# Key products shared between VectorE and GpSimd, initial states written behind the products, five pair buffers for the values, and attention outputs in the banks of the scores

## The chip, the cores and the metric

The kernel runs on one core of one Trainium2 chip. A core has a matrix engine (TensorE, PE in the profile; its weight loads are listed apart as PEld), a vector engine (VectorE, DVE), an activation engine (ScalarE, ACT), a general engine (GpSimd, POOL) and a queue that here issues all transfers (SyncE, SP). They run side by side, each works through its own instructions in order, and they meet through semaphores. SBUF is the on-chip memory of 128 partitions; matmul results land in PSUM, of which the kernel's four pools take 2 + 4 + 1 + 1 banks. The metric is the time of one execution on the device in microseconds (us).

## The reference, cut to what matters

Two layers follow each other on 16 sequences of 112 tokens of width 512.

```
# layer 0: cross-attention, 16 heads of 32, context of 375 rows
a = layer_norm(ctx);  Q, K, V = x @ Wq.T, a @ Wk.T, a @ Wv.T
x = x + tanh(gate) * (softmax(Q @ K.T * scale, masked) @ V) @ Wo.T

# layer 1: recurrence with a 16 x 16 state per head, 32 heads
xk, xw, xv, xr, xg = five token-shift mixes of layer_norm(x)
w = exp(-exp(decay(xw)));  r, k, v, g = projections of xr, xk, xv, xg
for t:  out_t = r_t . (u * k_t v_t^T + s);   s = k_t v_t^T + w_t[:, None] * s
x1 = x + (group_norm(out) * silu(g)) @ Wo.T
out = x1 + sigmoid(mix_r @ Wfr.T) * (relu(mix_k @ Wfk.T)**2 @ Wfv.T)
```

What matters here is the loop over `t`. The state starts from rows of the context (`s0`), each step adds the outer product of keys and values, and the output reads the state with `r`.

## The kernel before, in words

The 16 sequences form four groups (g) of four, 448 columns each. Two Python generators are woven into one program. `attention()` makes the first layer for all groups, and `recurrent(g)` the second for one group. The recurrence yields numbers, and after each the attention is advanced by as much work as `FILL[g]` times that number (1.2, 1.2, 0.9 and 0.0). The last group runs without attention beside it. TensorE's order is this program's order. The other engines' orders are laid down by the framework's planner, which may put an instruction of theirs ahead of another one of the program.

**Attention.** Per sequence b and quarter m of the heads, `scores` (L217) takes four banks of the pool `ps_s`, which has four, and writes four score tiles (L231). VectorE adds the mask and takes the minimum (L241, one instruction per head with its accumulator read), ScalarE does the exponential (L244). One round later `transposed` (L250) turns the weights in three pieces through the same pool (L254, copies L260 and L262), and one round after that `outputs` (L265) multiplies them with the values (L272) and ScalarE copies the result (L276). Units of other work (context transposes, keys, values, query and output projections) are put between. All these, and `outputs` too, take their bank from the pool `ps_mm`, which has two.

**Recurrence.** After layer norm and mixes a group has 16 steps n: four chunks c of 128 features by four pieces e. The decay products of a chunk are put in a PSUM tile (L507). In a step every partition holds one (head, i) pair, and the four rows q of a buffer hold four j. The columns are time, so the recurrence is a scan along the columns:

- `spread(n)` (L516): four transfers (L524) read value rows back from DRAM and broadcast each to 16 partitions, 223.5 KB each. Then ScalarE copies the initial states into the first column of each sequence (L528).
- `scans(n)` (L532): for each pair of rows VectorE multiplies the values with the keys in place (L544), scans each row (L548), and GpSimd multiplies the pair with the receptances (L552).
- `summed(n)` (L556): TensorE sums over i (L562), and every fourth time the result goes on (L568).

The buffers of four rows are two for the values (`kva`, `kvb`) and two for the states (`sta`, `stb`), taken by n % 2. In the loop the order was: the scans of step n, a projection of chunk c + 1, the spread of n + 1, the sums of n - 1, and the group norm pieces `centred`, `scaled`, `gated` of chunk c - 1.

Projections take their weights from a pool of slabs (L101), eight deep, loaded by the same SP queue as the spreads, the context (L91), the mask row (L221) and the value rows' way out to DRAM (L483).

## Time and profile before

| | |
|---|---|
| median of 3 runs | 1715.88 us (1714.5 to 1718.19) |
| the profiled execution's own time | 1713.49 us |
| its span | 1711.6 us |
| TensorE busy | 1417.8 us (83%) |
| VectorE busy | 960.9 us (56%) |
| ScalarE busy | 602.8 us (35%) |
| GpSimd busy | 442.3 us (26%) |
| mean granted TensorE clock | 0.902 |
| key products (L544) | 128 instructions, 94.0 + 99.3 us |
| scans (L548) | 256 instructions, 130.9 + 130.2 us |
| receptance products (L552) | 128 instructions, 144.5 + 141.0 us |
| initial-state copies (L528) | 64 instructions, 7.0 + 6.9 us |

The steps of the four groups lie at about 355 to 550, 750 to 955, 1150 to 1340 and 1490 to 1627 us. Before 355 there is attention alone, then the first layer norm and mixes. Between the others lie the end of one group, the feed-forward part and the start of the next, with attention between. A row of a timeline gives start, duration, engine, line, operation and operands, and in brackets the idle time of the engine before it with what ended it. A row of waits gives the sum, the number of times and the longest.

### The profile page before, as it was taken

The numbers are of one execution on the slowest core, as the hardware profiler recorded it, in microseconds if no ns is written. First come the engines' busy times: TensorE is split into PE (matmuls) and PEld (weight loads), VectorE is DVE, ScalarE is ACT, GpSimd is POOL, SyncE is SP. The second block draws the span as 40 slices with busy tenths as digits, with TensorE's granted clock in tenths as the row PEclk, the third lists the DMA queues.
The fourth block names the chain that finished last, engine by engine and source line by source line (L and its number), as shares of the span: only waits on it lengthen the run. The fifth ranks groups of instructions, "written<-read, shape, count | busy, mean of one in ns | idle before, by whom it ended". The sixth has DMA issues, their size and how long they took to land.

```text
span 1711.6 us, 17731 instructions
## 1 busy us (share of the span) xinstructions
PE 1417.8 (83%) x6272; PEld 701.5 (41%) x6272; DVE 960.9 (56%) x1660; ACT 602.8 (35%) x1324; POOL 442.3 (26%) x290
## 2 busy tenths in 40 slices
PE   6899999887878889897787889988777987967658
PEld 3455554443333454444343445444332543422124
DVE  1244333668766252549777333467877543599932
ACT  2455454423343352433333442342232532112231
POOL 0000001323434111123354110223444120355510
PEclk9899999999988989998998989988798998889689
DMA  7100010043321113014332012104332112144211
GB/s 220 59 20 20 20 48 22 20 126 106 118 95 54 57 49 111 20 32 136 117 117 90 29 55 85 37 18 149 116 106 84 33 50 76 55 161 146 90 37 46
DMA packets 74887, 129.61 MB, mean 76 GB/s; under 512 B 7680, under 2 KB 47616, under 8 KB 74544
## 3 DMA queue, kind: packets, MB, share of 16 engines
q1 hardware_dynamic: 74800, 128.50, 23.7%
q8 instruction: 49, 0.80, 0.2%
q14 instruction: 38, 0.31, 0.1%
HBM read 121.13 MB, written 7.34 MB: 75 GB/s over the span
## 4 chain that ended last, share of the span: by engine, by line
PE 47%; DVE 22%; DMA 17%; ACT 7%; issue 5%; POOL 2%; SPq 1%; DVEq 0%; ACTq 0%; POOLq 0%
PE pv L180 8%; DMA ctx<-in_ctx 6%; PE pk L170 5%; DMA kvb<-vd 5%; DVE stb L548 5%; DVE sta L548 5%; DMA kva<-vd 4%; PE pfk L122 3%; PE pfv L122 3%; PE pfr L122 3%; PE po L122 3%; ACT pr L244 3%; PE pt L254 3%; PE pq L122 3%; PE pp L122 2%
## 5 line engine op out<-in xcount | busy, mean ns | idle before, releaser
L170 PE MATMUL pk<-aT,wk 128*128 128x375 f32 x512 | 204.3, 549 | 29.5 <-DVE qT L297 11.2
L552 POOL TENSOR_TENSOR sta<-sta,r 128x896 f32<-128x896 f32 x64 | 144.5, 2271 | 250.0 <-DVE sta L548 245.9
L180 PE MATMUL pv<-wv,aT 128*125 128x512 f32 x384 | 190.3, 644 | 22.1 <-DVE o L573 6.2
L552 POOL TENSOR_TENSOR stb<-stb,r 128x896 f32<-128x896 f32 x64 | 141.0, 2220 | 156.6 <-DVE stb L548 156.6
L244 ACT ACTIVATE pr<-pr,mn 112x375 f32<-112x375 f32 x256 | 152.3, 596 | 71.9 <-DVE mn L241 71.4
L241 DVE CUSTOM_DVE_ANT_0 pr<-ps,mb 112x375 f32<-112x375 f32 x256 | 126.4, 542 | 76.8 <-PE ps L231 76.5
L170 PEld LDWEIGHTS pk<-aT,wk 128*128 128x128 f32 x512 | 107.7, 220 | 103.2 <-issue 27.0
L254 PEld LDWEIGHTS pt<-ident,pr 112*125 112x125 f32 x768 | 110.2, 206 | 64.3 <-issue 34.8
L548 DVE TENSOR_TENSOR_SCAN stb<-wp,kvb 128x448 f32<-128x448 f32 x128 | 130.2, 1068 | 9.3 <-PE acc L562 9.3
L548 DVE TENSOR_TENSOR_SCAN sta<-wp,kva 128x448 f32<-128x448 f32 x128 | 130.9, 1070 | 5.3 <-ACT kva L528 5.3
L254 PE MATMUL pt<-ident,pr 112*125 112x112 f32 x768 | 119.0, 294 | 15.7 <-DVE xm L441 15.7
L544 DVE TENSOR_TENSOR kva<-kva,k 128x888 f32<-128x888 f32 x64 | 94.0, 1475 | 45.7 <-DMA kva<-vd 45.1
L180 PEld LDWEIGHTS pv<-wv,aT 128*125 128x125 f32 x384 | 74.7, 204 | 108.9 <-issue 83.3
L544 DVE TENSOR_TENSOR kvb<-kvb,k 128x888 f32<-128x888 f32 x64 | 99.3, 1561 | 23.8 <-DMA kvb<-vd 23.7
L445 POOL TENSOR_TENSOR xm<-xm,xa 128x448 f32<-128x448 f32 x48 | 56.3, 1194 | 179.2 <-DVE xm L441 175.2
L262 DVE COPY prT<-pt 125x448 f32<-125x448 f32 x80 | 49.4, 617 | 86.6 <-PE pt L254 86.4
L231 PE MATMUL ps<-kT,qT 32*112 32x375 f32 x512 | 79.9, 552 | 16.5 <-ACT prT L260 11.1
L260 ACT COPY prT<-pt 125x448 f32<-125x448 f32 x112 | 59.3, 530 | 87.8 <-PE pt L254 87.8
L156 PE MATMUL pa<-ident,ctx 125*128 125x125 f32 x192 | 39.4, 323 | 54.9 <-DVE ctx L141 16.9
L135 DVE BATCH_NORM_STATS2 st<-ctx 125x6 f32<-125x512 f32 x48 | 31.2, 677 | 92.1 <-DMA ctx<-in_ctx 92.1
L175 ACT COPY kT<-pk 128x375 f32<-128x375 f32 x64 | 30.0, 469 | 127.4 <-PE pk L170 127.4
L223 POOL TENSOR_SCALAR mb<-mrow 112x375 f32<-112x375 uint8 x16 | 10.7, 671 | 246.5 <-DVE mn L241 163.9
(143 smaller groups left out, 2158.2 us busy)
## 6 DMA issues: line engine op xcount, KB each, us to landing
kva<-vd SPq DMA_DIRECT2D x128, 223.5 KB
kvb<-vd SPq DMA_DIRECT2D x128, 223.5 KB
ctx<-in_ctx SPq DMA_DIRECT2D x16, 750.0 KB
wo<-in_wo SPq DMA_DIRECT2D x32, 256.0 KB
wq<-in_wq SPq DMA_DIRECT2D x16, 256.0 KB
wv<-in_wv SPq DMA_DIRECT2D x16, 256.0 KB
wk<-in_wk SPq DMA_DIRECT2D x16, 256.0 KB
wr<-in_wr SPq DMA_DIRECT2D x16, 256.0 KB
```

The costliest lines, as they stand in the source:

```text
L122: nc.tensor.matmul(ps[:, :N], w[:, k, :], rhs[:, k, :], start=(k == 0), stop=(k == NC - 1))
L170: nc.tensor.matmul(pk[:, :S], wk[:, k, m * P : (m + 1) * P], aT[:, k, :], start=(k == 0), stop=(k == NC - 1),)
L180: nc.tensor.matmul(pv[:SC, :], aT[:, k, c * SC : (c + 1) * SC], wv[:, k, :], start=(k == 0), stop=(k == NC - 1),)
L231: nc.tensor.matmul(ps[:T, :S], qT[r : r + HD, m, t0 : t0 + T], kT[r : r + HD, :], start=True, stop=True,)
L241: nc.vector.tensor_tensor_reduce(pr, pss[hh][:T, :S], mb, 1.0, 3.0e38, ALU.add, ALU.min, mn)
L244: nc.scalar.activation(pr, pr, AF.Exp, bias=mn, scale=-1.0, accum_out=dens[b][:, h : h + 1])
L254: nc.tensor.transpose(pt[:SC, hh * T : (hh + 1) * T], prs[hh][:, c * SC : (c + 1) * SC], ident[:T, :T])
L260: nc.scalar.copy(prT, pt[:SC, :N])
L445: engine.tensor_tensor(xm[f][:, c, :], xm[f][:, c, :], xa[:, c, :], ALU.add)
L544: nc.vector.tensor_tensor(pair, pair, k_prev.unsqueeze(1).broadcast_to([P, 2, GB, T - 1]), ALU.mult)
L548: nc.vector.tensor_tensor_scan(st[:, q, :], w_ps[c], kv[:, q, :], 0.0, ALU.mult, ALU.add)
L552: nc.gpsimd.tensor_tensor(pair, pair, rs[c].unsqueeze(1).broadcast_to([P, 2, N]), ALU.mult)
```

## The change

- The slabs are six deep instead of eight.
- `outputs` takes its bank from `ps_s` instead of `ps_mm`.
- The value buffers are cut to pairs: two from `kva`, two from `kvb`, and a fifth, `kvc`. Step n uses pairs 2n and 2n + 1, modulo five.
- `spread` issues transfers only. The initial states are no longer copied by ScalarE.
- A new `products(n)` multiplies the first pair of a step on VectorE and the second on GpSimd, each followed on the same engine by a copy of its initial states into the first columns.
- `scans(n)` has no products any more.
- In the loop the spread of n + 1 comes before the scans of n, and the products of n + 1 come after the projection, where the spread was.

```diff
-    slabs = pool("slabs", 8)
+    slabs = pool("slabs", 6)
...
-        po = mm_tile(f"po_{b}_{m}")
+        po = ps_s.tile([P, 512], F32, tag="s", name=f"po_{b}_{m}")
...
-        kvs = [wide("xa", f"kva_{g}"), wide("kv", f"kvb_{g}")]
+        kva, kvb = wide("xa", f"kva_{g}"), wide("kv", f"kvb_{g}")
+        kvc = big.tile([P, 2, N], F32, tag="kvc", name=f"kvc_{g}")
+        kvs = [kva[:, 0:2], kva[:, 2:4], kvb[:, 0:2], kvb[:, 2:4], kvc]
...
-            kv = kvs[n % 2]
...
             for q in range(NQ):
+                kv = kvs[(2 * n + q // 2) % len(kvs)]
                 nc.sync.dma_start(
-                    kv[:, q, 1:N],
+                    kv[:, q % 2, 1:N],
...
-            nc.scalar.copy(
-                kv.rearrange("p q (b t) -> p q b t", t=T)[:, :, :, 0], s0[:, c, e : NS : NQ, :]
-            )
+        def products(n):
+            c, e = divmod(n, NQ)
+            k_prev = ks[c].rearrange("p (b t) -> p b t", t=T)[:, :, 0 : T - 1]
+            for p, engine in enumerate((nc.vector, nc.gpsimd)):
+                kv4 = kvs[(2 * n + p) % len(kvs)].rearrange("p q (b t) -> p q b t", t=T)
+                engine.tensor_tensor(
+                    kv4[:, :, :, 1:T], kv4[:, :, :, 1:T],
+                    k_prev.unsqueeze(1).broadcast_to([P, 2, GB, T - 1]), ALU.mult,
+                )
+                engine.tensor_copy(
+                    kv4[:, :, :, 0], s0[:, c, 8 * p + e : 8 * p + e + 5 : NQ, :]
+                )
...
-            for q0 in (0, 2):
-                pair = kv4[:, q0 : q0 + 2]
-                nc.vector.tensor_tensor(
-                    pair, pair, k_prev.unsqueeze(1).broadcast_to([P, 2, GB, T - 1]), ALU.mult
-                )
-                for q in (q0, q0 + 1):
+            for p in range(2):
+                kv = kvs[(2 * n + p) % len(kvs)]
+                for q in range(2):
...
         spread(0)
+        products(0)
         for n in range(NQ * NC):
...
+            if n + 1 < NQ * NC:
+                spread(n + 1)
             scans(n)
...
             if n + 1 < NQ * NC:
-                spread(n + 1)
+                products(n + 1)
```

## The prediction

> **What bounds the kernel now.** I read the page's slices first, then busy time by stage, then waits, then single rows. The slices show TensorE nearly full, with its clock sagging where the scans run.

> ```profile
> PE   6899999887878889897787889988777987967658
> ...
> PEclk9899999999988989998998989988798998889689
> ```

> By stage (columns: stretch, its length, busy time and count of PE, PEld, DVE, ACT, POOL, granted clock, transfers' share, GB/s):

> ```profile
> 60.00:300.00 240.00, 222.53 (x1321) 126.92 (x1322) 95.71 (x285) 118.02 (x291) 13.61 (x21) 0.95 0.09 27
> 355.00:550.00 195.00, 153.89 (x703) 73.16 (x702) 150.47 (x207) 69.53 (x159) 77.43 (x37) 0.88 0.32 106
> 550.00:750.00 200.00, 176.44 (x808) 91.85 (x806) 79.96 (x192) 80.18 (x172) 36.97 (x36) 0.96 0.17 52
> 750.00:955.00 205.00, 166.57 (x759) 80.57 (x759) 151.30 (x215) 71.66 (x165) 78.86 (x38) 0.88 0.32 103
> ...
> 1150.00:1340.00 190.00, 152.81 (x654) 70.95 (x652) 141.28 (x185) 59.38 (x138) 78.72 (x41) 0.87 0.32 104
> 1490.00:1627.00 137.00, 93.92 (x246) 29.78 (x247) 132.24 (x118) 28.87 (x55) 70.59 (x34) 0.81 0.41 134
> ```

> TensorE idles 41, 38 and 37 us in the first three groups' steps (rows 2, 4, 5), 117 us together, at a clock of 0.87 to 0.88. In row 1 it idles 7%. The last group's steps are VectorE's: 132 of 137 us busy, and from 1490.0 to 1626.6 us it makes 16 steps of 8.54 us. So the change is worth what it does to TensorE's waits in three stretches and to VectorE's chain in the fourth. Who is late in the three stretches?

> ```profile
> ACT kva L528 <- DMA kva<-vd: 130.9, 26, 9.4
> ...
> ACT kvb L528 <- DMA kvb<-vd: 113.9, 26, 6.6
> ```

> ScalarE stands 245 us at the head of an initial-state copy, waiting for value rows, with its other work behind. Two ScalarE rows and two TensorE rows of the timeline show what that costs:

> ```profile
> 830.07 0.22 ACT L528 COPY kva<-s 128x16 f32<-128x16 f32 x1 [7.29 <-DMA kva<-vd]
> 830.18 0.53 ACT L481 COPY v<-pv 128x448 f32<-128x448 f32 x1
> ...
> 826.34 0.76 PE L272 MATMUL po<-prT,v 125*32 125x112 f32 x24
> 830.76 4.18 PE L170 MATMUL pk<-aT,wk 128*128 128x375 f32 x8 [3.66 <-ACT v L481]
> ```

> The value eviction L481 sits behind the copy, its bank stays taken, TensorE stops 3.66 us, and its next eight matmuls take 4.18 us where the same row elsewhere takes 2.70.

> **ScalarE's copies go.** 64 copies of 0.22 us free 14 us of an engine with room: nothing by itself. The wait counts. I laid each TensorE stall of the three stretches over ScalarE's waits for value rows: they overlap for 14, 13 and 11 us, 38 together. The rest of the 117 us hangs on exponentials, on VectorE, on context loads. I take three quarters, since another late engine often stands behind the first: -28. From below nothing is gained if ScalarE's next item is late too; from above 38 plus some 10 of backlog worked off after the wait. [...] By the rows, 473 us of busy TensorE times (1 - 0.88/0.90) is 10.5 us for two hundredths of clock. [...]

> **Outputs in the score banks.** Gain: the output copy L276, late behind four exponentials, no longer holds one of two `ps_mm` banks. TensorE waits for it 27 us in the three stretches (6 already in the 38) and 17 us elsewhere. I take -8 and -15. Loss: per round the score pool is now asked for 4 + 1 + 3 banks, with four there, so the outputs want the bank of the round's first scores, and cannot start before VectorE has read it:

> ```profile
> 127.24 0.90 PE L231 MATMUL ps<-kT,qT 32*112 32x375 f32 x8
> 128.06 0.78 PE L272 MATMUL po<-prT,v 125*32 125x112 f32 x24
> ...
> 128.15 0.55 DVE L241 CUSTOM_DVE_ANT_0 pr<-ps,mb 112x375 f32<-112x375 f32 x1 [3.63 <-PE ps L231]
> ```

> Here outputs start at 128.06 and the read ends at 128.70: a new wait of 0.64 us, with an idle VectorE. Going through all 62 outputs so, the read ends later than the start by 61 us in sum: 28 outside the three stretches, 33 inside. Behind the waiting outputs is the whole of TensorE. Outside I count all, +28, as nothing covers it. Inside, about half falls on stalls there already (the 5.2 us at 826.34 meets the 3.66 us above): +14. Bounds: 0 and 33, more if VectorE gets later.

> **Products and states, spread earlier, five pairs.** VectorE loses 64 products and gains 64 copies of 8 elements; GpSimd gains 64 products and 64 copies. The prices:

> ```profile
> L544 DVE TENSOR_TENSOR kva<-kva,k x64: 1048/1084/2996, 360.1 to 1612.9; 128x888 f32<-128x888 f32 x64
> ...
> L552 POOL TENSOR_TENSOR sta<-sta,r x64: 2070/2082/2926, 366.1 to 1618.2; 128x896 f32<-128x896 f32 x64
> ...
> L141 DVE TENSOR_SCALAR ctx<-ctx,mv,rs x48: 533/542/2300, 16.2 to 1148.2; 125x512 f32<-125x512 f32 x48
> ```

> A product is 1.05 us on VectorE when free, and 2.07 on GpSimd by L552, of the same kind and nearly the same size; its broken rows might make it 2.5. Small copies: 0.16 us on VectorE (by L402, 128x4), 0.2 on GpSimd (by L283, 203 ns). The maxima above are 1.8 to 1.9 us over the minima: VectorE has stood behind GpSimd for most of a GpSimd instruction. [...] By the uncontended rows the last group's step on VectorE would be 4.02 (scans) + 1.05 + 0.16 + about 1.2 (others) = 6.4 us, a saving of 16 x 2.1 = 34. [...] I take 8.35: 16 x (8.54 - 8.35) = -3, between -34 and +6. [...]

> In the first three groups a step takes 12 us, so both engines have room. VectorE sheds 25 us of products per group and up to 21 us of waits for rows, since a pair's transfers now wait for scans 1.5 to 2 steps back instead of one, and rows take 3 to 6.5 us to land in the chain's entries. It pays with about 1.5 us per small copy shut out and 1 us per step for GpSimd's product. I call that even: 0, from -20 to +30. GpSimd's product can queue behind the receptance products, the gate product (L593), mask and spread work (L223, L287), and VectorE's third scan waits for it. Behind that scan sits L241, and behind L241 the exponentials and outputs. Behind the first product on VectorE stand the same.

> **Queues.** The four transfers of a spread (3.5 us of SP when issued together) move ahead of a slab load and, once per chunk, of the value rows' way out (L483), which is due four steps later. With six slabs, a load would go out when the sixth projection back has ended; over all 160 projections the nearest still leaves 14.9 us before first use. Such a load moves 256 KB, a spread 894 KB in about 5 us, so it is there in time: 0. POOL's queue issues no transfer.

> **Sum.** -28 - 6 - 8 + 14 - 15 + 28 - 3 = -18, on the profiled 1713.5 us: 1695.5. The median shown is 2.4 us above that execution, so **1698 us**. Its own range, with the halves I took varied, is 1680 to 1712.

> **Rivals.** (a) Outputs wait longer (slower, **1740**). One mechanism: VectorE reaches L241 later, since GpSimd shuts it out more. If all 61 us count and no bank wait is saved, the sum is -28 - 6 + 61 - 3 = +24. It turns slower once the outputs' waits cost 37 us net. For it: 33 us inside the stretches arise with VectorE 77% busy. Against: VectorE's waits for rows, part of that lateness, should go. [...] (c) The stalls fall much further (**1670**), as the coupling of ScalarE, VectorE and TensorE dissolves: 28 us more. For: the stretches between idle 11 to 12%. Against: a third of the stalls has no part in the value rows.

> **Chances.** Forecast 0.42, (a) 0.26, (b) 0.15, (c) 0.17. This kernel's measurement tells about 0.2% (3.4 us) from no change. Faster: 0.36 + 0.01 + 0.03 + 0.17 = 0.57; same: 0.04 + 0.03 + 0.04 = 0.11; slower: 0.02 + 0.22 + 0.08 = 0.32. The range leaves out the ends of (a) and (c): **1655 to 1745**.

> **What would show it.** Right: no ScalarE wait for `kva` or `kvb`; TensorE idle near 28 us per stretch at a clock near 0.90; L272 waiting for L241 some 0.6 us in quiet rounds; GpSimd about 160 us busier. Wrong: L272 waiting over 60 us in all; L548 waiting for GpSimd in most steps; the last group's step far from 8.35 us; a transfer of slabs in TensorE's waits.

## The result: no measurable change

The changed kernel takes 1711.35 us (median of 20 executions, 1697.12 to 1721.35) and the kernel before, beside it, 1712.85 us (1706.84 to 1720.83). The ratio is 0.9986 with a 95% interval of 0.9965 to 1.0007. The prediction had 1698 us and a clear gain as the likeliest case. The profiled execution took 1710.53 us, with a span of 1708.6 us and a mean granted clock of 0.901.

The gain was not absent, it was given back. The same stretches as before, in columns of the same order (stretch, length, busy time and count of PE, PEld, DVE, ACT and POOL, granted clock, share of the transfers, GB/s); the stretches are shifted to the changed kernel's own steps:

```profile
60.00:300.00 240.00, 212.78 (x1241) 121.13 (x1242) 91.22 (x273) 113.78 (x278) 13.26 (x20) 0.95 0.09 26
364.00:559.00 195.00, 160.10 (x720) 76.14 (x720) 136.16 (x208) 70.15 (x147) 112.41 (x70) 0.87 0.33 107
...
754.00:959.00 205.00, 168.83 (x758) 80.98 (x757) 137.70 (x215) 70.41 (x147) 112.33 (x70) 0.86 0.31 103
...
1487.00:1624.00 137.00, 96.25 (x266) 32.84 (x266) 118.41 (x118) 27.47 (x41) 114.17 (x66) 0.85 0.44 141
```

In the quiet stretch TensorE is now idle 27.2 us instead of 17.5. In the steps (second and third row) it is idle 35 and 36 us, with the clock lower than before (0.87 and 0.86 against 0.88), where about 28 us and 0.90 were expected. In the last group VectorE is busy 118 us and GpSimd 114, and the same 137 us hold 20 matmuls more.

The waits of the changed kernel (engine, line and tile, what it waited for: sum, times, longest):

```profile
PE po L272 <- DVE mn L241: 77.1, 38, 7.1
...
POOL kva L538 <- DMA kva<-vd: 72.6, 9, 20.5
...
DVE kva L538 <- DMA kva<-vd: 34.7, 14, 5.0
DVE kvb L538 <- DMA kvb<-vd: 30.6, 9, 5.7
...
DVE kvc L542 <- DMA kvc<-vd: 15.3, 3, 5.4
```

ScalarE's 245 us for value rows are gone, as forecast. But VectorE's waits for rows, which were to fall, rose from 69 us to 105 us (all its lines for `kva`, `kvb` and `kvc` together), and the outputs' new wait for L241 is 77 us, over the 60 that the prediction named as a sign against it. Three rows of the changed kernel's timeline for VectorE and two for TensorE show one place where both occur:

```profile
829.46 2.04 DVE L542 COPY kvb<-s 128x8 f32<-128x8 f32 x1
...
833.93 1.08 DVE L538 TENSOR_TENSOR kvc<-kvc,k 128x888 f32<-128x888 f32 x1 [2.35 <-DMA kvc<-vd]
...
835.00 0.54 DVE L241 CUSTOM_DVE_ANT_0 pr<-ps,mb 112x375 f32<-112x375 f32 x1
...
835.60 1.35 PE L272 MATMUL po<-prT,v 125*32 125x112 f32 x24 [6.85 <-DVE mn L241]
836.88 4.36 PE L170 MATMUL pk<-aT,wk 128*128 128x375 f32 x8
```

VectorE spends 2.04 us on a copy of 8 elements and stands 2.35 us at the head of a product whose rows have not landed. L241 is the next of its instructions that matter to TensorE; it starts at 835.00, and the outputs at 835.60, after 6.85 us without work on TensorE. So the wait for rows is a third of this stall. Whether it is what costs the time, the experiments have to tell.

### The profile page after: what moved, and what is told of

It is laid out like the page before. It is cut to its first block, busy times and chain, and to the rows that moved or that the text cites. A ratio compares the mean times of both kernels' runs of the same rounds, so it can differ in the third digit from the quotient of the medians.

```text
span 1708.6 us, 17672 instructions
## 1 busy us (share of the span) xinstructions
PE 1413.5 (83%) x6272; PEld 697.1 (41%) x6272; DVE 904.6 (53%) x1660; ACT 594.1 (35%) x1260; POOL 584.5 (34%) x418
## 4 chain that ended last, share of the span: by engine, by line
PE 49%; DVE 21%; DMA 18%; ACT 5%; issue 4%; POOL 3%; SPq 1%; DVEq 0%; POOLq 0%; ACTq 0%
DMA ctx<-in_ctx 7%; PE pv L180 7%; PE pk L170 6%; DVE sta L557 5%; DVE stb L557 4%; DMA kvb<-vd 4%; PE pfk L122 3%; PE pfv L122 3%; PE pfr L122 3%; DMA kva<-vd 3%; PE po L122 3%; PE pp L122 3%; PE pq L122 3%; PE pt L254 2%; PE ps L231 2%
## 5 line engine op out<-in xcount | busy, mean ns | idle before, releaser
L170 PE MATMUL pk<-aT,wk 128*128 128x375 f32 x512 | 207.3, 556 | 23.9 <-DVE qT L297 13.5
L180 PE MATMUL pv<-wv,aT 128*125 128x512 f32 x384 | 175.8, 603 | 5.2 <-DVE g L601 4.3
L561 POOL TENSOR_TENSOR stb<-stb,r 128x896 f32<-128x896 f32 x64 | 137.1, 2163 | 75.8 <-DVE stb L557 73.9
L241 DVE CUSTOM_DVE_ANT_0 pr<-ps,mb 112x375 f32<-112x375 f32 x256 | 126.3, 540 | 65.6 <-PE ps L231 65.6
L170 PEld LDWEIGHTS pk<-aT,wk 128*128 128x128 f32 x512 | 108.5, 222 | 100.0 <-issue 29.0
L254 PEld LDWEIGHTS pt<-ident,pr 112*125 112x125 f32 x768 | 106.4, 199 | 66.5 <-issue 36.4
L272 PE MATMUL po<-prT,v 125*32 125x112 f32 x1536 | 58.1, 291 | 77.9 <-DVE mn L241 77.1
L180 PEld LDWEIGHTS pv<-wv,aT 128*125 128x125 f32 x384 | 69.5, 189 | 83.1 <-issue 74.3
L223 POOL TENSOR_SCALAR mb<-mrow 112x375 f32<-112x375 uint8 x16 | 10.0, 628 | 252.8 <-DVE mn L241 165.8
L538 POOL TENSOR_TENSOR kva<-kva,k 128x888 f32<-128x888 f32 x28 | 58.0, 2072 | 99.5 <-DMA kva<-vd 72.6
L272 PEld LDWEIGHTS po<-prT,v 125*32 125x32 f32 x1536 | 40.4, 121 | 122.7 <-DVE mn L241 114.2
L231 PE MATMUL ps<-kT,qT 32*112 32x375 f32 x512 | 80.8, 563 | 9.6 <-DVE prT L262 6.1
L571 PE MATMUL acc<-sta,consts 128*32 128x448 f32 x256 | 46.9, 658 | 32.9 <-POOL sta L561 16.5
L122 PE MATMUL pr<-xm,wr 128*128 128x448 f32 x128 | 63.2, 646 | 6.1 <-DVE o L582 6.1
```

Of the source, the lines that this page charges most:

```text
L122: nc.tensor.matmul(ps[:, :N], w[:, k, :], rhs[:, k, :], start=(k == 0), stop=(k == NC - 1))
L170: nc.tensor.matmul(pk[:, :S], wk[:, k, m * P : (m + 1) * P], aT[:, k, :], start=(k == 0), stop=(k == NC - 1),)
L180: nc.tensor.matmul(pv[:SC, :], aT[:, k, c * SC : (c + 1) * SC], wv[:, k, :], start=(k == 0), stop=(k == NC - 1),)
L231: nc.tensor.matmul(ps[:T, :S], qT[r : r + HD, m, t0 : t0 + T], kT[r : r + HD, :], start=True, stop=True,)
L241: nc.vector.tensor_tensor_reduce(pr, pss[hh][:T, :S], mb, 1.0, 3.0e38, ALU.add, ALU.min, mn)
L254: nc.tensor.transpose(pt[:SC, hh * T : (hh + 1) * T], prs[hh][:, c * SC : (c + 1) * SC], ident[:T, :T])
```

## The experiments

The recorded expectations give theories letters, in the order in which they were formed, and say in words what each holds: first the outputs' new wait, then GpSimd's share and the small copies that it shuts out, last (D) the fifth pair and VectorE's order. "The run with the outputs back" is the first experiment.

To place a difference, each span is cut at TensorE's milestones: a group's steps run from its first value projection of the recurrence to the first matmul of its output projection. The steps of the first three groups are added up; the rest is the span less all four groups' steps. Single profiles differ by some 5 us in a stage, so verdicts go by the ratios. Each ratio is to executions of the kernel before on the same chip, so medians of two rows are not set against each other; a difference of ratios is turned into us with 1713 us.

| kernel | median us | ratio to before, 95% | span | steps of groups 1 to 3 | last group | rest | VectorE's waits for rows |
|---|---|---|---|---|---|---|---|
| before | 1712.85 | 1 | 1711.6 | 658.2 | 156.5 | 897.0 | 69 |
| changed | 1711.35 | 0.9986 [0.9965, 1.0007] | 1708.6 | 644.8 | 147.1 | 916.7 | 105 |
| e1 outputs back | 1686.10 | 0.9849 [0.9808, 0.9890] | 1685.7 | 650.4 | 146.8 | 888.5 | 110 |
| e2 outputs alone | 1722.38 | 1.0052 [1.0032, 1.0073] | 1720.4 | 645.2 | 156.9 | 918.3 | 71 |
| e3 products on VectorE | 1712.28 | 1.0010 [0.9988, 1.0032] | 1705.0 | 631.6 | 160.9 | 912.5 | 43 |
| g1 states behind, alone | 1680.23 | 0.9838 [0.9811, 0.9866] | 1676.4 | 633.8 | 156.9 | 885.7 | 44 |
| f1 four pairs, outputs back | 1664.46 | 0.9737 [0.9701, 0.9773] | 1669.6 | 630.7 | 147.4 | 891.5 | 36 |
| h2 changed, four pairs | 1684.63 | 0.9836 [0.9809, 0.9862] | 1682.1 | 616.3 | 147.9 | 917.9 | 42 |
| f6 order held, one step | 1649.77 | 0.9652 [0.9627, 0.9677] | 1650.7 | 613.4 | 147.2 | 890.1 | 11 |
| f7 order held behind scans | 1670.74 | 0.9775 [0.9750, 0.9801] | 1666.5 | 622.1 | 156.2 | 888.2 | 8 |
| f8 changed, held | 1679.63 | 0.9824 [0.9803, 0.9846] | 1677.7 | 600.8 | 157.8 | 919.1 | 7 |
| f9 four pairs, held | 1676.54 | 0.9776 [0.9750, 0.9803] | 1675.5 | 625.6 | 154.1 | 895.8 | 8 |
| f10 f6 + last copies on ScalarE | 1645.44 | 0.9611 [0.9585, 0.9637] | 1646.3 | 615.1 | 140.3 | 890.9 | 9 |
| f11 f10 + outputs in steps | 1634.65 | 0.9586 [0.9559, 0.9612] | 1628.8 | 597.1 | 140.3 | 891.4 | 7 |

### Outputs back in the shared banks

```diff
-        po = ps_s.tile([P, 512], F32, tag="s", name=f"po_{b}_{m}")
+        po = mm_tile(f"po_{b}_{m}")
```

> The changed kernel with one edit undone: the outputs take their bank from the two-bank pool again. Theory A (the outputs' wait for VectorE ate the gain): the 77 us in which TensorE waits for L241 before the outputs go, some 25 to 35 us of waits for the output copy come back, and the kernel falls to 1665 to 1690 us. Theory B (the wait for the value rows only moved from ScalarE to VectorE and GpSimd, so nothing was won to be eaten): only the quiet rounds gain, 10 to 15 us, 1697 to 1702 us, and TensorE still idles 33 us or more in each of the first three groups' steps.

Ratio 0.9849, against 0.9986 with the outputs in the score banks: this edit alone costs the changed kernel 0.0137 of 1713 us, 23 us. The `po` wait for L241 is gone from its waits, and the rest of the span falls from 916.7 to 888.5 us. Theory A's range holds, but not its place: the steps do not get shorter (644.8 to 650.4 us), and TensorE still idles over 42 us in each, as B has it.

### The outputs' edit alone, on the kernel before

The same line, the other way, in the kernel before.

> The kernel before with one edit: the outputs in the score banks. Theory A: slower by 20 to 45 us, 1733 to 1758 us, with over 60 us of waits of the outputs for L241. Theory B: slower by the quiet rounds' share, about 10 us, 1720 to 1725 us, since inside the steps TensorE was stopped anyway.

Ratio 1.0052, 9 us slower, as theory B had it. The new wait is the same as in the changed kernel, though VectorE makes all products here and GpSimd's share is the old one:

```profile
PE po L272 <- DVE mn L241: 78.8, 38, 7.7
```

So the 77 us of waiting in the changed kernel do not come from GpSimd's products. The stages show where it costs: the rest grows by 21 us, while the steps take 13 us less.

### All products on VectorE

```diff
-            for p, engine in enumerate((nc.vector, nc.gpsimd)):
+            for p, engine in enumerate((nc.vector, nc.vector)):
```

> The changed kernel with both products and both small copies on VectorE. Theory C (GpSimd shutting VectorE out costs as much as VectorE sheds): within 5 us of the changed kernel in the first three groups, the small copies seldom over 0.2 us. Against C: VectorE's extra 25 us of products per group make the first three groups' steps longer, 1720 to 1735 us in all. Either way the last group's steps go from 147 us back to 155 us or more.

Ratio 1.0010: no difference from the changed kernel that these intervals show. Two things cancel. The last group takes 13.8 us more, so GpSimd's half does pay there. The steps of the other groups take 13 us less although VectorE has 48 products more there, and its waits for rows are 43 us instead of 105. That pointed away from shutting out and toward the waits.

### States behind the products, alone

```diff
-            nc.scalar.copy(
-                kv.rearrange("p q (b t) -> p q b t", t=T)[:, :, :, 0], s0[:, c, e : NS : NQ, :]
-            )
...
                     pair, pair, k_prev.unsqueeze(1).broadcast_to([P, 2, GB, T - 1]), ALU.mult
                 )
+                nc.vector.tensor_copy(
+                    kv.rearrange("p q (b t) -> p q b t", t=T)[:, q0 : q0 + 2, :, 0],
+                    s0[:, c, 4 * q0 + e : 4 * q0 + e + 5 : NQ, :],
+                )
```

> The kernel before with one edit: the initial states are copied by VectorE behind each pair's product instead of by ScalarE ahead of it; everything else as before. My prediction's term for ScalarE's wait and the clock was -34 us: 1675 to 1685 us if it is right. Theory B (the wait for rows is VectorE's too, and only moves): 1700 us or more, since VectorE already stands at these rows with its products and TensorE's stalls inside the steps end a little later at the next engine.

Ratio 0.9838, 28 us faster with this one edit. It is the gain that the prediction put first, in its total. In its parts it is not: TensorE's idle time in the steps of groups 1 to 3 falls by 11 us only (127 to 115), its busy time there by 13, and the rest of the span is 11 us shorter, which is not clear of the scatter between profiles. VectorE's waits for rows fall as well, from 69 to 44 us.

### Four pairs instead of five

```diff
-        kvc = big.tile([P, 2, N], F32, tag="kvc", name=f"kvc_{g}")
-        kvs = [kva[:, 0:2], kva[:, 2:4], kvb[:, 0:2], kvb[:, 2:4], kvc]
+        kvs = [kva[:, 0:2], kva[:, 2:4], kvb[:, 0:2], kvb[:, 2:4]]
```

With the outputs back in the shared banks:

> The kernel with the outputs back in their own banks, and four pair buffers instead of five. Theory D (with five pairs the planner puts products and small copies up to two steps ahead of their scans, where VectorE stands for rows not due yet and in front of L241): VectorE's waits for value rows fall well below the 110 us of the five-pair form, and the time falls by 5 to 15 us, to 1671 to 1681 us. Against D: the rows are asked for half a step later and arrive later, VectorE and GpSimd wait more, 1690 to 1700 us.

In the changed kernel itself:

> The changed kernel with four pair buffers instead of five and nothing else. Theory D (the fifth pair lets the planner put products two steps ahead, and VectorE stands there): faster than the changed kernel by what the four pairs gave with the outputs back, 10 to 20 us, 1690 to 1702 us, with VectorE's waits for value rows well under 105 us. Against D (the gain belonged to that other placing): 1705 to 1715 us.

A buffer less is faster in both settings: 0.9737 against 0.9849 (19 us) and 0.9836 against 0.9986 (25 us). TensorE's order of instructions is the same row by row. What moves are the waits; with four pairs GpSimd waits longer for rows and VectorE shorter (first kernel):

```profile
POOL kva L537 <- DMA kva<-vd: 104.8, 22, 26.4
...
DVE kva L537 <- DMA kva<-vd: 20.5, 12, 2.4
DVE kvb L537 <- DMA kvb<-vd: 15.3, 11, 2.6
```

GpSimd's 150 us of waiting cost nothing that is seen; with VectorE's 110 goes the longer time. The order of instructions suggests why. VectorE's products (P), copies of states (C) and scans (S) of steps 0 to 5 in the first group, with the number of L241 rows between (two for each head, with the accumulator read):

```
planner's order, five pairs:  P0 C0 S0 P1 C1 P2 S1 [4] C2 P3 [4] C3 C4 P4 S2 [8] P5 C5 S3 ...
held to one step (f6):        P0 C0 S0 P1 C1 P2 S1 [4] C2 P3 [4] C3 S2 [6] P4 [2] C4 S3 P5 C5 S4 ...
held behind scans (f7):       P0 C0 S0 P1 C1 S1 P2 [6] C2 [2] S2 [6] P3 [2] C3 S3 ...
```

A fifth pair comes free earlier, so the planner puts P4 ahead of S2. Counted in the trace of the changed kernel, by how many scans have started before a product, 32 of VectorE's 48 products in the first three groups stand more than one step ahead of their own scans, and 66 of the 73 us for which these 48 wait lie before those 32. With four pairs none stands so far ahead. This was still a reading; the next three runs change the order and keep the five pairs.

### VectorE's order held

The first lets a product stand at most one step ahead, the second and third put it behind the last scan of the step before. The edges set the order of issue on VectorE only. Five pairs and their transfers stay, the first two with the outputs back. In the trace of the first, against the run with the outputs back, 78 of VectorE's 1660 rows stand elsewhere in the order, 7 of GpSimd's 418, 3 of ScalarE's 1260, one transfer and no matmul. Under the stricter hold more follows: in the third, against the changed kernel, 34 of GpSimd's rows and 13 transfers stand elsewhere as well.

```diff
         def products(n):
+            behind = last_scan.get(n - 2)      # n - 1 in the second and third
+            if behind is None:
+                products_of(n)
+            else:
+                with tc.issue_after(behind.ins):
+                    products_of(n)
+
+        def products_of(n):
...
-                    nc.vector.tensor_tensor_scan(
+                    last_scan[n] = nc.vector.tensor_tensor_scan(
```

> The changed kernel with the outputs back in the shared banks and five pair buffers, with one thing more: on VectorE each product and its copy are put behind the last scan of two steps earlier in the order of instructions, so that a product stands at most about one step ahead of its own scans. Transfers, buffers and GpSimd's half are as in the run with the outputs back (1686.1 us, ratio 0.985). Theory D (the fifth pair costs because the planner then puts VectorE's products up to two steps ahead, and VectorE stands for rows just asked for): VectorE's waits for rows fall from about 105 us to near 60 and the ratio to 0.975 to 0.982. Rival (the fifth pair costs through its earlier transfers or its place in memory, not through VectorE's order): the ratio stays at 0.983 to 0.988.

> As the run before, but each product of VectorE is put behind the last scan of the step just before its own, as the program's text has it. Theory D: VectorE's waits for rows are 30 to 50 us, as with four pairs (35.8 us, ratio 0.974), and the ratio is 0.970 to 0.979. Rival (not VectorE's order): 0.983 to 0.988. If the waits fall and the time doesn't, the waits were not what the fifth pair costs.

> The changed kernel itself, outputs in the banks of the scores and five pair buffers, with each product of VectorE put behind the last scan of the step just before its own. Theory D: about 20 to 28 us less than the changed kernel, ratio 0.982 to 0.988 (with four pairs it was 0.984). Rival (not VectorE's order): the changed kernel's own 0.997 to 1.001.

Held to one step: 0.9652 instead of 0.9849, 34 us from the order alone, more than expected. In the changed kernel itself the stricter hold gives 0.9824 instead of 0.9986, 28 us. The waits of the first of them:

```profile
DVE kva L547 <- DMA kva<-vd: 7.1, 4, 2.4
...
DVE kvc L547 <- DMA kvc<-vd: 3.5, 1, 3.5
...
POOL kva L547 <- DMA kva<-vd: 57.9, 8, 25.6
```

VectorE's waits for rows fall from 110 to 11 us. The stretches of the first group's steps and the second's, first in the run with the outputs back, then in the kernel held to one step:

```profile
348.20:569.84 221.64, 175.85 (x826) 86.38 (x825) 138.00 (x223) 81.66 (x169) 115.24 (x74) 0.92 0.31 100
747.38:974.46 227.08, 180.78 (x825) 87.80 (x824) 138.66 (x223) 82.21 (x169) 114.93 (x74) 0.89 0.30 98
```

```profile
347.36:560.84 213.48, 175.71 (x826) 85.64 (x825) 154.00 (x223) 82.07 (x169) 121.50 (x74) 0.92 0.32 104
736.99:950.33 213.34, 175.68 (x825) 86.30 (x824) 154.56 (x223) 82.22 (x169) 120.82 (x74) 0.92 0.32 104
```

Each stage holds the same matmuls (825 or 826 in the trace) and is 8 and 14 us shorter. TensorE's idle time falls from 46 to 38 us in both. Over the steps of the first three groups it falls from 135 to 109 us, and TensorE's busy time from 516 to 505. The hold in the changed kernel does the same: idle time 113 to 88 us, busy time 532 to 513. So the order costs about 25 us of waiting in both settings, and the rest is busy time at a lower clock: 0.92, 0.89 and 0.87 in the three groups' steps with the outputs back and 0.92 in each when held, 0.88, 0.87 and 0.89 in the changed kernel and 0.92, 0.93 and 0.90 when held.

The wait that pays is not the outputs' wait for L241, though. In the changed kernel with the hold it is as long as ever (77.1 us without):

```profile
PE po L272 <- DVE mn L241: 84.4, 37, 6.8
```

TensorE's other waits for VectorE's results, in the steps of the first three groups, fall from 62 to 32 us there, and from 67 to 50 us with the outputs back.

VectorE is busier, not less busy (154 against 138 us), because the small copies are shut out more often: their median, which is 0.27, 0.30 and 0.38 us in the three buffers with the outputs back, rises to 1.6 to 2.0 us. So shut-out copies are not what the first three groups pay for.

The stricter hold keeps most of the gain in these groups, but the last group, whose pace VectorE and GpSimd set, takes 156 instead of 147 us: there a product must be ahead. With four pairs the same hold gains nothing (0.9776, next run, against 0.9737), so what it removes is what the fifth pair brought.

### Four pairs with the order held

> Outputs back in the shared banks, four pair buffers instead of five, and VectorE's products held behind the last scan of the step before their own, so that VectorE's order no longer depends on when a pair comes free. Set beside the same hold with five pairs (1670.74 us, ratio 0.9775). Theory D in its strong form (the fifth pair costs only through VectorE's order): with the order fixed four pairs are no faster, ratio 0.976 to 0.985. Rival (the fifth pair costs in itself, through earlier transfers or its place in memory): four pairs stay clearly faster, 0.965 to 0.973.

Ratio 0.9776, and 0.9775 with five pairs under the same hold. VectorE's order is the same in both traces, row by row. With it fixed the buffer costs and gives nothing that these intervals (some 4 us to each side) show. What the fifth pair cost was the order that it allowed.

Under the looser hold the fifth pair seems to pay. Four pairs in the planner's order also have no product more than one step ahead, at 0.9737 and with 36 us of waits for rows; five pairs held to one step have 0.9652 and 11 us. The two differ in 66 of VectorE's rows as well, so these 15 us are not the buffer's alone.

### Where the small copies count

Three kernels move products or copies. Products and copies on VectorE in the first three groups, shared in the last (outputs back, five pairs):

```diff
-            for p, engine in enumerate((nc.vector, nc.gpsimd)):
+            for p, engine in enumerate((nc.vector, nc.gpsimd if g == NG - 1 else nc.vector)):
```

> The kernel with the outputs back in their own banks, and both products and copies on VectorE in the first three groups, shared with GpSimd in the last group alone. Theory C (in the first three groups GpSimd shutting VectorE out costs more than the products it takes): the 13 us that this saved in the first three groups with the outputs in the score banks are saved again, 1670 to 1677 us. Against C: that saving belonged to the outputs' wait, and without it the time stays at 1683 to 1690 us.

1670.31 us, ratio 0.9775 [0.9738, 0.9812]: 13 us less than with shared products in these groups' steps (637.5), with VectorE's waits for rows at 43 us. It fits the order as the cause as well as GpSimd's share.

All small copies on GpSimd, outputs back:

```diff
-                engine.tensor_copy(
+                nc.gpsimd.tensor_copy(
```

> The kernel with the outputs back, five pairs, and all initial-state copies on GpSimd. Theory C (shutting out): VectorE loses 64 copies that took 57 us with the standing behind GpSimd, 40 us over their own 0.17 us each, and the time falls by 5 to 12 us, to 1674 to 1681 us. Against C: the first pair's scans now wait for GpSimd's copy behind its products, and the time rises, 1688 to 1700 us.

1689.48 us, ratio 0.9851 [0.9812, 0.9890]. Nothing is gained: VectorE no longer stands behind GpSimd with a copy, and waits 127 us for rows instead of 110.

All small copies on ScalarE, outputs back (`nc.scalar.copy` in the same place):

> The kernel with the outputs back in their own banks, and the initial states copied by ScalarE as before, behind the products. Prediction's step (ScalarE standing at these copies stops TensorE): slower by 15 to 34 us than the same kernel with the copies on VectorE and GpSimd, 1700 to 1720 us. Theory C: VectorE no longer stands 64 times behind a GpSimd product for a copy of 8 elements, some 50 us of its time, so it is no slower, 1680 to 1690 us.

1674.43 us, ratio 0.9811 [0.9770, 0.9853], so not slower than with the copies on VectorE and GpSimd (0.9849). ScalarE waits 257 us for rows again, as in the kernel before, and the steps of the first three groups do not get longer (646.5 us against 650.4). In this setting, where VectorE is late too, ScalarE's standing costs nothing that shows. The last group takes 140.4 us instead of 146.8. So one kernel put the parts together in the last group only, on four pairs in the planner's order:

> All that helped, together: outputs in their own banks, four pairs, both products and copies on VectorE in the first three groups, and in the last group products shared with GpSimd and copies on ScalarE. From the stages of the runs before: 1656 to 1666 us. If the parts do not add (the first three groups bounded by another engine by now), 1666 to 1674 us.

1681.16 us, ratio 0.9820 [0.9789, 0.9851]: slower than four pairs alone (0.9737), with the loss in the first three groups' steps (648 against 631 us). With the products of these groups all on VectorE its waits for rows were 52 instead of 36 us, which is too little for 17 us. Why these parts did not add is open. With the order held, the last part did add:

```diff
-                engine.tensor_copy(
+                copy = nc.scalar.copy if g == NG - 1 else engine.tensor_copy
+                copy(
```

> The kernel with the outputs back, five pairs and products held to one step ahead (1649.77 us, ratio 0.965), with one thing more: in the last group alone, which has no attention beside it, ScalarE makes the copies of the initial states. If the copies that GpSimd shuts out set the last group's pace, as when all copies were on ScalarE (last group 140.4 us against 147), the last group loses 6 to 7 us and the ratio is 0.960 to 0.963. If GpSimd's own work sets it, nothing changes: 0.964 to 0.967. Since TensorE's order is the same, the first three groups should stay as they are.

The last group falls from 147.2 to 140.3 us, the first three stay, and the ratio is 0.9611 (0.9652 without). The intervals overlap slightly, the stage is the one named. The edit also takes 16 copies off GpSimd in that group, 3.6 us of its time. With all copies on GpSimd the last group took 143.9 us instead of 146.8, so VectorE's shut-out copies account for some 3 of the 7 us, and for the rest the two engines' copies are not told apart. In the first three groups moving all copies gave 3 to 4 us, which is within the scatter.

### Slabs alone

`pool("slabs", 6)` instead of 8, in the kernel before.

> The kernel before with six slabs instead of eight. The prediction put nothing down for it, since every load still had 14.9 us left: within 0.3% of the kernel before. If loads do come late, TensorE waits for slab loads and it is slower by 5 us or more.

1712.79 us, ratio 1.0003 [0.9988, 1.0019]: nothing.

### Outputs in the score banks during the steps only

The four pairs of runs that differ in the outputs' banks alone agree in their stages (score banks less shared banks, us):

| pair | steps of groups 1 to 3 | rest |
|---|---|---|
| e2 less before | -13 | +21 |
| changed less e1 | -6 | +28 |
| h2 less f1 | -14 | +26 |
| f8 less f7 | -21 | +31 |

```diff
-        po = mm_tile(f"po_{b}_{m}")
+        po = (ps_s.tile([P, 512], F32, tag="s", name=f"po_{b}_{m}")
+              if in_steps else mm_tile(f"po_{b}_{m}"))
...
+        in_steps.append(g)
         spread(0)
         products(0)
...
             yield 1.5
+        in_steps.clear()
         yield 5
```

> The fastest kernel so far (1645.44 us, ratio 0.961: outputs in the shared banks, five pairs, products held to one step ahead, the last group's copies on ScalarE) with one thing more: outputs take the banks of the scores while a group's 16 steps run, and the shared banks at all other times. In four pairs of runs that differ in the outputs' banks alone the steps of the first three groups together took 6 to 21 us less with the score banks and the rest of the span 22 to 31 us more. If the two sides are separate, the steps fall by 6 to 20 us and the rest stays near 891 us: ratio 0.950 to 0.958. Rival (the two belong together, the outputs of one stage pushing the next one's): the rest grows by as much, 0.960 or above.

1634.65 us, ratio 0.9586, between the two expectations and not resolved from 0.9611 by the time. The stages decide: steps 18 us less (597.1), rest the same (891.4). Gain and loss are separate. It has the lowest ratio of all runs, 4.1% under the kernel before.

## Why the prediction was wrong

**The step that failed** is "Products and states, spread earlier, five pairs", with its "I call that even: 0", and in it the term "up to 21 us of waits for rows" that VectorE would shed because transfers start earlier. VectorE's waits rose instead, from 69 to 105 us. The step took VectorE's order from the program's text, where the products of n + 1 follow the scans of n. The text before the prediction says that the planner may move instructions ahead, and a pair that is free sooner is what lets it. A product placed two steps ahead stands for rows just requested, with all of VectorE's later work behind it. Cost of the fifth pair: +25 us (0.9986 against 0.9836), shown to be the order by the held runs (28 us in the changed kernel) and by four and five pairs being equal once held. The reason itself was not wrong: with five pairs held to one step the waits are 11 us.

How the order reaches TensorE is shown in part. The hold takes 25 us of idle time from TensorE in the steps of the first three groups, most of it in waits for VectorE other than the outputs' wait for L241. Which of these waits follows from which product was not tried. The prediction looked for trouble at L241, and that wait came, but from the outputs' own edit.

Taking -28 for the states, +23 for the outputs and -9 for the last group out of the measured -2 leaves about +12 us for the whole step. So the fifth pair's +25 hid some 13 us that the rest of the step gave.

The other steps, by their numbers:

- **ScalarE's wait, -28, and clock, -6.** Alone it gave -28 us (0.9838) where the two terms had -34. The total is near, the parts are luck: 11 us of idle time in the three stretches instead of 28, and the rest in busy time and outside. That ScalarE's standing is what costs is not shown: with all copies on ScalarE it stood 257 us and the kernel was no slower. No run shows the clock's -6 either: the rows that the prediction gives come to 10.5 us for two hundredths of clock, and in the steps of the first three groups the clock is 0.91, 0.90 and 0.90 with the edit alone and 0.88, 0.87 and 0.89 in the changed kernel, against 0.90, 0.90 and 0.88 before. Stalls over 3.4 us number 13 in the three stretches before, 11 in the changed kernel and 11 in the kernel held to one step, where the clock is 0.92: the count of long stalls doesn't tell the clock here. The last section says what the traces show instead.
- **Outputs in the score banks, +19.** Alone +9, in place +23: the sum was about right, by luck, since its halves were not. Inside the steps the prediction had -8 + 14 = +6, and the runs show -6 to -21. Outside it had -15 + 28 = +13, and they show +21 to +31. The loss outside was put at 0.64 us per output with an idle VectorE; in the quiet stretch from 60 to 300 us it is 15 waits with 16.2 us in all, 1.1 us each. Rival (a) named the right wait, and 77 us of it came, but against a gain inside the steps, so 1740 was far off.
- **Last group, -3.** It took 9.3 us less (156.5 to 147.1), 0.58 us a step. The GpSimd product is 2.07 us, as priced by L552, and not the 2.5 that its broken rows might have made it:

```profile
L538 POOL TENSOR_TENSOR kva<-kva,k 128x888 f32<-128x888 f32 x28 | 58.0, 2072 | 99.5 <-DMA kva<-vd 72.6
```

  No run shows the step of 8.35 us that the -3 is taken from, nor its bound of +6. GpSimd is busy 115.9 us over the 16 steps, 7.2 us each, and a step takes 7.73. In the whole kernel VectorE's scans wait for GpSimd's half five times, 6.4 us together.
- **Slabs 0, queues 0.** Slabs alone made no difference; the earlier transfers cost nothing once VectorE's order was held (0.9776 in f9 against 0.9775 in f7).
- **Left over.** Four pairs in the changed kernel (-28) less ScalarE's -28, outputs +17 (what they cost with four pairs, 0.9836 against 0.9737) and last group -9 leave -8, or -14 with the outputs' +23 of five pairs. It belongs to GpSimd's half and the new order in the first three groups. No run separates these two.

Of the signs to look for, those for ScalarE, GpSimd (142 us busier, about 160 expected) and the slabs came as written; the others did not: TensorE idles 36 to 39 us in a group's steps and not 28, the clock fell below 0.90, L272 waits over 60 us, and the last group's step, from first scan to first scan, is 7.73 us (8.41 before by the same measure) and not 8.35.

## What to carry to other kernels

An extra buffer is also a licence: where a planner lays down an engine's order, it lets a consumer be placed as early as its buffer is free, and an in-order engine then waits for a transfer that was just issued, with everything else behind it (in the changed kernel 66 of the 73 us for which VectorE's products of the first three groups wait). So price a new buffer by where the consumer will stand in the order, and if it is to be early for the transfer alone, hold the consumer back: held to one step ahead gave 34 us here, held to none 13. Check which wait the hold removes: the most visible one here, the outputs' 77 us, stayed while the time fell by 28. Cut the effect of an edit by stages before adding it up; an edit with a small total (the outputs' banks) may be a gain in one stage and a loss in another, and can be kept in the one alone.

## What the runs showed of the hardware

Copies of 8 elements per partition on VectorE took 0.14 to 0.17 us at the shortest, by buffer, and up to 2.04 us in the changed kernel, where a GpSimd product takes 2.07. Each of its 25 copies over 1 us, of 64, ended 0.03 us after the end of a GpSimd instruction. Two groups of them (minimum, median and maximum in ns), then a group of the same copy in the kernel held to one step:

```profile
L542 DVE COPY kvb<-s x24: 156/287/2043, 377.8 to 1607.1; 128x8 f32<-128x8 f32 x24
L542 DVE COPY kvc<-s x12: 167/175/2041, 385.9 to 1589.6; 128x8 f32<-128x8 f32 x12
```

```profile
L551 DVE COPY kvb<-s x24: 157/2034/2056, 370.1 to 1548.3; 128x8 f32<-128x8 f32 x24
```

The prediction had read such standing, 1.8 to 1.9 us, off the longest rows of the kernel before, and the full 1.9 us is there. The trace of that kernel bears the reading out: each of the 42 products on VectorE (L544) over 1.3 us, of 128, ended 0.94 us after the end of a GpSimd instruction. What was not expected is how little it matters: 42 us of copy time over its own in the changed kernel (0.7 us a copy, where the prediction had 1.5) and 81 in the far faster held one. Only where VectorE and GpSimd set the pace, in the last group, did it show in the time, with 3 to 7 us.
